# Newton statistics of a Stieltjes attention placed in PSUM instead of SBUF

## The chip, the cores and the metric

The kernel runs on one core of a Trainium2 chip, in one launch. The metric is the device time of that launch in microseconds (us); before the change it is 5724.81 us, the median of three runs (5724.38 to 5730.4).

## What is computed

The reference has two parts that follow each other. `x` is 8 sequences of 512 tokens with 128 channels, all in float32.

```python
x = x + _L0_attn_ref(_layernorm(x), Wqkv, Wo)        # first part: 16 heads of 8 channels
x = x + _L0_ffn_ref(_layernorm(x), ...)              # second part: 6 layers, local attention and MLP
...
def stieltjes_attention(Q, K, V, scale, causal, q, num_iter):   # q = 1, num_iter = 4
    s = jnp.einsum('bhnd,bhmd->bhnm', Q, K) * scale
    s_masked = jnp.where(mask, s, -1e+30)
    lam = s_masked.max(-1) + 1.0
    for _ in range(num_iter):
        d = jnp.maximum(lam[..., None] - s, EPS)
        w = jnp.where(mask, d ** (-q), 0.0)
        f = w.sum(-1) - 1.0
        fp = -q * jnp.where(mask, d ** (-q - 1.0), 0.0).sum(-1)
        lam = lam - f / fp
    d = jnp.maximum(lam[..., None] - s, EPS)
    p = jnp.where(mask, d ** (-q), 0.0)
    p = p / p.sum(-1, keepdims=True)
    return jnp.einsum('bhnm,bhmd->bhnd', p, V)
```

So each row of the scores needs a root of `sum(1/(lam - s)) = 1`, found with four Newton steps. A step needs two sums over the row: that of `w = 1/d` and that of `w*w`. Only the first part is touched by the change.

## The kernel before

The kernel is written for a tile framework. The program text gives the work in an order of priority; a scheduler decides at build time in which order each engine gets its instructions, and puts semaphore waits where two instructions touch the same data. For tiles in PSUM it takes two accesses to one bank of a tile as touching each other, whichever columns they use. The order on an engine is then fixed, and the engine works through it in sequence.

**The first part** works on blocks of 128 rows of one sequence. A block `rb` (0 to 3) sees `W = (rb + 1) * 128` columns. Blocks are taken in pairs, (3, 0) and (2, 1), so 16 pairs in all for 8 sequences. A pipeline over the pairs has three stages: while the pair `nxt` gets its scores, the pair `now` gets its Newton steps and the pair `before` gets its weights and sums of V. In each turn the loops over `k` (4 Newton steps) and `u` (the two blocks of a pair) call, in this order, `attend_add` (L264), `scores` (L195), `newton` (L225), `attend_sum` of the turn before (L275) and `attend_weigh` (L269). There are 16 x 4 x 2 = 128 calls of `newton` and 128 of `attend_sum`.

- `scores` makes a score tile with TensorE (L204), and VectorE adds the mask and takes the row minimum (L209); L215 and L217 make the distances `ns` in SBUF.
- `newton` makes `w` for four groups `j` of four heads: ScalarE takes Ln (L234, L237 or L241) and Exp with scale -1 (L242) into `d`, a pool of two buffers. For the narrow blocks GpSimd adds the growth `dl` of `lam` first (`add_growth`, L222). VectorE then takes `bn_stats` of each head (L244): 16 a call, each writing count, mean and sum of squared deviations for the even and the odd elements, six numbers. L249 to L260 turn them into the new `dl` with eight or nine small VectorE instructions on 16 or 32 elements for each partition; the ninth (L259) runs only for `k > 0`, so 3 calls in 4.
- `attend_add` is again the GpSimd line L222, on a tile `da`; `attend_weigh` makes the weights (ScalarE L269, L270) and masks the diagonal (GpSimd L272).
- `attend_sum` transposes the weights with TensorE (L286), copies them to SBUF with VectorE (L288, `dT`, one copy for each of four heads), multiplies with V on TensorE (L293) into a PSUM tile `po` with a bank of its own, and copies that out with VectorE (L297). A block with `nkb = rb + 1` column blocks has `4 * nkb` such multiplications; the profile shows two matmuls for each[...].

All operands of L249 to L260 lie in SBUF before the change. The eight PSUM banks of the first part are taken: four for scores, two for transposes, one for projections, one for `po`.

**The second part** (from L326 on) runs the six layers. Nothing in it changes.

Of the kernel before, what the change touches and what calls it, by code (L numbers as in the profile page):

```python
# [9 lines left out]
F32 = mybir.dt.float32  # L10
BF16 = mybir.dt.bfloat16
AF = mybir.ActivationFunctionType
ALU = mybir.AluOpType
AX = mybir.AxisListType
PSUM = bass.MemoryType.PSUM

P = 128
N = 512
# [4 lines left out]
H = 16  # L23
# [26 lines left out]
def tile_kernel(  # L50
# [18 lines left out]
    nc = tc.nc  # L69
# [20 lines left out]
    def normalized_T(pool, ppool, b, dst):  # L90

        st = pool.tile([P, NT, 6], F32, name="st")
        mv = pool.tile([P, NT, 2], F32, name="mv")
        for c in range(NT):
            nc.vector.bn_stats(st[:, c, :], x2[:, b, c, :])
            nc.vector.bn_aggr(mv[:, c, :], st[:, c, :])
        rstd = pool.tile([P, NT], F32, name="rstd")
        nc.scalar.activation(rstd, mv[:, :, 1], AF.Ln, bias=eps_ln)
        nc.scalar.activation(rstd, rstd, AF.Exp, scale=-0.5)
        xn = pool.tile([P, NT, D], F32, name="xn", bufs=1)  # L100
        pt = ppool.tile([P, N], F32, name="pt", tag="misc")
        for c in range(NT):
            nc.vector.tensor_scalar(
                xn[:, c, :], x2[:, b, c, :], mv[:, c, 0:1], rstd[:, c : c + 1],
                ALU.subtract, ALU.mult,
            )
            nc.tensor.transpose(pt[:, c * P : (c + 1) * P], xn[:, c, :], ident)
        nc.scalar.copy(dst, pt)


    with ExitStack() as c1:
# [5 lines left out]
        sm = c1.enter_context(tc.tile_pool(name="sm", bufs=4))  # L117
# [3 lines left out]
        ps_o = c1.enter_context(tc.tile_pool(name="ps_o", bufs=1, space=PSUM))  # L121
# [99 lines left out]
        def add_growth(d, ns, dl, j):  # L221
            nc.gpsimd.tensor_tensor(  # L222
                d, ns, dl[:, 4 * j : 4 * j + 4].unsqueeze(2).to_broadcast(list(d.shape)), ALU.add
            )

        def newton(t, k):
            W, dl = t["W"], t["dl"]

            st = sm.tile([P, H, 2, 3], F32, name="stw")
            for j in range(4):  # L230
                ns = t["ns"][j]
                d = dp.tile([P, 4, W], F32, name="d", tag="d")
                if k == 0:
                    nc.scalar.activation(d, ns, AF.Ln)  # L234
                elif W <= 2 * P:
                    add_growth(d, ns, dl, j)
                    nc.scalar.activation(d, d, AF.Ln)  # L237
                else:
                    for g in range(4):
                        i = 4 * j + g  # L240
                        nc.scalar.activation(d[:, g, :], ns[:, g, :], AF.Ln, bias=dl[:, i : i + 1])  # L241
                nc.scalar.activation(d, d, AF.Exp, scale=-1.0)  # L242
                for g in range(4):
                    nc.vector.bn_stats(st[:, 4 * j + g].rearrange("p u k -> p (u k)"), d[:, g, :])  # L244

            hw = float(W // 2)
            mean = st[:, :, :, 1]
            q2 = sm.tile([P, H, 2], F32, name="q2")
            nc.vector.scalar_tensor_tensor(q2, mean, hw, mean, ALU.mult, ALU.mult)  # L249
            nc.vector.tensor_tensor(q2, q2, st[:, :, :, 2], ALU.add)  # L250
            sw2 = sm.tile([P, H], F32, name="sw2")
            nc.vector.tensor_tensor(sw2, q2[:, :, 0], q2[:, :, 1], ALU.add)
            sw = sm.tile([P, H], F32, name="sw")
            nc.vector.tensor_tensor(sw, mean[:, :, 0], mean[:, :, 1], ALU.add)
            nc.vector.tensor_scalar(sw, sw, hw, -1.0, ALU.mult, ALU.add)
            nc.vector.reciprocal(sw2, sw2)
            nc.vector.tensor_tensor(sw, sw, sw2, ALU.mult)
            if k > 0:
                nc.vector.tensor_tensor(sw, sw, dl, ALU.add)  # L259
            nc.vector.tensor_scalar(dl, sw, 0.0, None, ALU.max)  # L260

        def attend_add(t, j):

# [13 lines left out]
        def attend_sum(t, d, j):  # L277

            nkb, (qj, kn, va) = t["nkb"], t["proj"]
            if j == 0:  # L280
                t["o4"] = bt.tile([P, 4, P], F32, name="o4")
            dT = []
            for g in range(4):
                pt = ps_t.tile([P, nkb, P], F32, name="dTp", tag="t")
                for kb in range(nkb):
                    nc.tensor.transpose(pt[:, kb, :], d[:, g, kb * P : (kb + 1) * P], ident)  # L286
                dT.append(tr.tile([P, nkb, P], F32, name="dT", tag="dT"))
                nc.vector.tensor_copy(dT[g], pt)  # L288

            po = ps_o.tile([P, P], F32, name="po")  # L290
            for kb in range(nkb):
                for g in range(4):
                    nc.tensor.matmul(  # L293
                        po[32 * g : 32 * g + 32, :], lhsT=va[:, kb, 4 * g + j, :],
                        rhs=dT[g][:, kb, :], start=(kb == 0), stop=(kb == nkb - 1),
                    )
            nc.vector.tensor_copy(t["o4"][:, j, :], po)  # L297
            if j == 3:
                attend_end(t)
                if t["rb"] == 1:  # L300
                    normalized_T(bt, ps_m, t["b"], xT[:, t["b"], :])

        def attend_end(t):
            b, rb, o4 = t["b"], t["rb"], t["o4"]
            pq = ps_m.tile([P, 4, 4, 32], F32, name="pq4", tag="misc")
            for j in range(4):
                nc.tensor.transpose(pq[:, j].rearrange("p g r -> p (g r)"), o4[:, j, :], ident)
            den = sm.tile([P, 4, 4], F32, name="den")
            nc.vector.reciprocal(den, pq[:, :, :, DH])
            o = bt.tile([P, H, DH], F32, name="o")  # L310
            nc.vector.tensor_tensor(
                o.rearrange("p (g j) d -> p j g d", j=4), pq[:, :, :, 0:DH],
                den.unsqueeze(3).to_broadcast([P, 4, 4, DH]), ALU.mult,
            )
            pT = ps_m.tile([P, P], F32, name="pT", tag="misc")
            nc.tensor.transpose(pT, o.rearrange("p h d -> p (h d)"), ident)
            oT = bt.tile([P, P], F32, name="oT")
            nc.scalar.copy(oT, pT)
            pr = ps_m.tile([P, P], F32, name="pr", tag="misc")
            nc.tensor.matmul(pr, lhsT=oT, rhs=wT[:, 3, :], start=True, stop=True)  # L320
            nc.vector.tensor_tensor(x2[:, b, rb, :], x2[:, b, rb, :], pr, ALU.add)
# [10 lines left out]
        for w in range(len(work) + 1):  # L332
            before, now, nxt = now, nxt, []
            if w + 1 < len(work):
                b, rbs = work[w + 1]
                nxt = [block(b, rb, proj) for rb in rbs]
            for k in range(NUM_ITER):
                for u in range(2):
                    if before:
                        attend_add(before[u], k)  # L340
                    if nxt:
                        scores(nxt[u], k)
                    if now:
                        newton(now[u], k)
                    if ready:
                        attend_sum(*ready)
                        ready = None
                    if before:
                        attend_weigh(before[u])
                        ready = (before[u], before[u]["d"], k)  # L350
            if w + 2 < len(work) and work[w + 2][1][0] == 3:
                if ready:
                    attend_sum(*ready)
                    ready = None
                proj = project(work[w + 2][0])
        attend_sum(*ready)


# [354 lines left out]
    while t < len(halves) * PH + LAG or parts:  # L713
        i, p = t // PH, t % PH
        a = done = ahead = None
        if 0 <= i < len(halves):
            a = dict(g=groups[i], p=p)
# [87 lines left out]
```

## Time and profile before

| what | value |
|---|---|
| median of three runs | 5724.81 us |
| the profiled execution's own time | 5724.38 us |
| its span, first to last instruction | 5722.4 us |
| busy share over the span: TensorE, VectorE, ScalarE, GpSimd | 82%, 83%, 71%, 57% |
| first part, about 0 to 2060 us: last Newton step's end | 2062.7 us |
| `bn_stats` L244: count, busy in the whole first part | 2048, 871 us (four shapes) |
| L249 to L260: instructions | 1120 |

PE stands for TensorE, DVE for VectorE, ACT for ScalarE, POOL for GpSimd. In the views of groups each row names line, engine, operation, the tile written and the tile read, shapes and count; behind the bar stand the busy time in us and the mean duration in ns, then the idle time just before, with what ended it. In a timeline a row is the start in us, the length in us, and the instructions; rows of several instructions are runs of equal ones, and a row can start before the one ahead of it has ended, because instructions overlap a little in the engine.

### The profile page before, as it was taken

What the parts mean: (1) busy time and instruction counts of PE and PEld (TensorE: products, weight loads), DVE (VectorE), ACT (ScalarE), POOL (GpSimd) and SP (SyncE); (2) the same over time, 40 slices, a digit from 0 to 9 for tenths busy, and PEclk for the clock granted to TensorE, in tenths of its full rate; (3) what the DMA queues carried; (4) which work ended last, traced back from release to release, by engine and by line L of the source; (5) the groups of instructions that cost most, each with busy time, mean ns of one, the idle gap of its engine ahead of it and who ended that gap; (6) DMA issues with size and microseconds to landing.
All of it is one profiled execution on the core that took longest, in us unless ns stands there. A gap on an engine that the chain in (4) does not pass through costs nothing.

```text
span 5722.4 us, 108133 instructions
## 1 busy us (share of the span) xinstructions
PE 4686.3 (82%) x40909; PEld 2744.5 (48%) x40909; DVE 4775.5 (83%) x12028; ACT 4038.0 (71%) x6458; POOL 3250.3 (57%) x2915
## 2 busy tenths in 40 slices
PE   4556566655666549999999999999999999999998
PEld 2223333332333225556656555555555655556665
DVE  8889898998989858888888888888888888888886
ACT  5788888888888856666666666666666666666665
POOL 1333233333323347777777677777777777777774
PEclk6555555555555569999999999999999999999999
DMA  0000000000000011111111211122111111121111
GB/s 17 1 0 1 1 1 1 1 1 0 1 1 1 1 39 44 44 47 47 46 44 42 58 47 40 39 51 53 44 44 44 52 44 42 47 58 45 47 42 34
DMA packets 106558, 173.16 MB, mean 30 GB/s; under 512 B 12816, under 2 KB 30008, under 8 KB 106040
## 3 DMA queue, kind: packets, MB, share of 16 engines
q1 hardware_dynamic: 106040, 166.25, 11.7%
q8 instruction: 325, 5.32, 0.4%
q14 instruction: 193, 1.58, 0.1%
HBM read 19.42 MB, written 2.10 MB: 4 GB/s over the span
## 4 chain that ended last, share of the span: by engine, by line
PE 39%; DVE 33%; ACT 20%; POOL 5%; issue 2%; DMA 0%; SPq 0%; POOLq 0%; ACTq 0%; DVEq 0%
DVE stw L244 9%; PE m L476 8%; PE po L594 4%; PE pT L584 4%; PE pv L512 4%; PE s L559 3%; ACT d L241 3%; ACT d L242 3%; DVE qr L492 3%; ACT qT L540 3%; DVE ss L482 3%; PE acc L607 3%; DVE rs L572 3%; DVE qn L484 3%; DVE ns L209 2%
## 5 line engine op out<-in xcount | busy, mean ns | idle before, releaser
L496 POOL TENSOR_TENSOR qn<-qn,qr 128x512 f32<-128x512 f32 x768 | 975.5, 1271 | 580.4 <-DVE qr L492 430.0
L244 DVE BATCH_NORM_STATS2 stw<-d 128x6 f32<-128x512 f32 (+3 forms) x2048 | 868.1, 476 | 76.7 <-ACT d L242 74.8
L504 POOL TENSOR_TENSOR qn<-qn,ss 128x512 f32<-128x512 f32 x768 | 784.6, 1042 | 40.5 <-ACT ss L501 36.8
L482 DVE TENSOR_REDUCE ss<-sq 128x8 f32<-128x512 f32 x768 | 522.2, 680 | 328.5 <-ACT sq L481 326.0
L574 POOL TENSOR_TENSOR pr<-pr,rs 128x768 f32<-128x768 f32 x384 | 564.0, 1469 | 382.9 <-DVE rs L573 249.1
L476 PE MATMUL m<-wqkv,xs 128*128 128x512 f32 x1536 | 738.4, 603 | 48.2 <-ACT qT L540 37.6
L222 POOL TENSOR_TENSOR d<-ns,dl 128x512 f32<-128x512 f32 (+1 forms) x192 | 288.1, 1500 | 641.6 <-DVE stw L244 388.8
L242 ACT ACTIVATE d<-d 128x1536 f32<-128x1536 f32 (+3 forms) x512 | 641.3, 1261 | 5.3
L204 PE MATMUL s<-kn,qj 32*128 32x512 f32 (+3 forms) x1024 | 420.0, 753 | 245.5 <-DVE mn L209 242.0
L572 DVE TENSOR_REDUCE rs<-pr 128x8 f32<-128x768 f32 x384 | 364.8, 950 | 287.7 <-ACT pr L570 287.5
L222 POOL TENSOR_TENSOR da<-ns,dl 128x2048 f32<-128x2048 f32 (+3 forms) x128 | 299.1, 2340 | 502.4 <-PE dTp L286 362.1
L492 DVE TENSOR_TENSOR qr<-m,tab 128x256 f32<-128x256 f32 x1536 | 571.2, 413 | 0.0
L286 PE MATMUL dTp<-ident,da 128*128 128x128 f32 x1280 | 382.4, 424 | 221.5 <-ACT da L270 107.4
L481 ACT ACTIVATE sq<-m 128x512 f32<-128x512 f32 x768 | 439.3, 601 | 129.3 <-PE m L476 83.1
L601 ACT COPY oT<-po 128x512 f32<-128x512 f32 x384 | 223.8, 583 | 413.5 <-PE po L594 407.9
L484 DVE TENSOR_TENSOR qn<-m,tab 128x512 f32<-128x512 f32 x768 | 514.7, 670 | 0.0
L540 ACT COPY qT<-ptq 128x512 f32<-128x512 f32 x768 | 416.5, 583 | 90.6 <-PE ptq L535 90.0
L585 ACT COPY prT<-pT 96x512 f32<-96x512 f32 x768 | 431.5, 584 | 62.6 <-PE pT L584 53.5
L293 PE MATMUL po<-dT,va 128*32 128x128 f32 x2560 | 333.5, 395 | 173.1 <-DVE dT L288 173.0
L535 PEld LDWEIGHTS ptq<-ident,qn 128*128 128x128 f32 x3072 | 358.8, 141 | 220.0 <-issue 111.5
L241 ACT ACTIVATE d<-ns,dl 128x512 f32<-128x512 f32 (+1 forms) x768 | 450.6, 654 | 14.2 <-DVE stw L244 14.2
L584 PE MATMUL pT<-ident,pr 128*96 128x128 f32 x3072 | 411.6, 274 | 55.8 <-DVE rs L573 46.2
(137 smaller groups left out, 9910.0 us busy)
## 6 DMA issues: line engine op xcount, KB each, us to landing
v<-v SPq DMA_DIRECT2D x192, 512.0 KB
v<-v SPq DMA_DIRECT2D x96, 256.0 KB
v<-v SPq DMA_DIRECT2D x96, 192.0 KB
wqkv<-in_L_ffn_Wqkv_dram SPq DMA_DIRECT2D x36, 256.0 KB
wo<-in_L_ffn_Wo_dram SPq DMA_DIRECT2D x12, 256.0 KB
x<-in_L_attn_x_dram SPq DMA_DIRECT2D x8, 256.0 KB
out_dram<-x SPq DMA_DIRECT2D x8, 256.0 KB
w<-in_L_ffn_W_dram SPq DMA_DIRECT2D x6, 341.0 KB
```

The lines of the kernel that those rows point to most:

```text
L222: nc.gpsimd.tensor_tensor(d, ns, dl[:, 4 * j : 4 * j + 4].unsqueeze(2).to_broadcast(list(d.shape)), ALU.add)
L241: nc.scalar.activation(d[:, g, :], ns[:, g, :], AF.Ln, bias=dl[:, i : i + 1])
L242: nc.scalar.activation(d, d, AF.Exp, scale=-1.0)
L244: nc.vector.bn_stats(st[:, 4 * j + g].rearrange("p u k -> p (u k)"), d[:, g, :])
L476: nc.tensor.matmul(m.rearrange("p h e -> p (h e)"), lhsT=lhsT, rhs=wqkv[:, t, :], start=True, stop=True,)
L482: nc.vector.tensor_reduce(ss[:, t, :], sq, axis=AX.X, op=ALU.add)
L484: nc.vector.tensor_tensor(qc, m, tab[:, 2 * t, c, :].unsqueeze(1).to_broadcast([P, HH, DHL]), ALU.mult)
L492: nc.vector.tensor_tensor(qr[:, :, u, :], mh[:, :, 1 - u, :], sw.unsqueeze(1).to_broadcast([P, HH, hd]), ALU.mult,)
L496: nc.gpsimd.tensor_tensor(qc, qc, qr.rearrange("p h u e -> p h (u e)"), ALU.add)
L504: nc.gpsimd.tensor_tensor(qc, qc, ss[:, t, :].unsqueeze(2).to_broadcast([P, HH, DHL]), ALU.mult)
L540: nc.scalar.copy(q, pt)
L584: nc.tensor.transpose(pT[:, c, :], pr[:, e, c, :], ident)
```

## The change

One PSUM tile `small` of a full bank (512 numbers for each partition) is allocated once, in the pool that held `po`. Its first 128 columns are `po`. Behind them lie two sets of statistics `st` and of two rows `r`, which calls of `newton` use in turn. `bn_stats` writes to `st` in PSUM. The small instructions are rewritten so that none has two tensor operands in SBUF, and none has two in PSUM: a copy of the means to SBUF comes first, the sums over the even and odd halves are reductions, and the reciprocal and the step go to `r` in PSUM. The number of small instructions stays at eight, nine for `k > 0`. The formulas are scaled by `1/hw` but give the same step.

```diff
+        small = ps_o.tile([P, N], F32, name="small")
+        po = small[:, 0:P]
+        stats, turn, c0 = [], 0, P
+        for u in range(2):
+            st = small[:, c0 : c0 + 6 * H].rearrange("p (h u k) -> p h u k", u=2, k=3)
+            r = small[:, c0 + 6 * H : c0 + 8 * H].rearrange("p (a h) -> p a h", h=H)
+            stats.append((st, r))
+            c0 += 8 * H
+
         def newton(t, k):
+            nonlocal turn
             W, dl = t["W"], t["dl"]
 
-            st = sm.tile([P, H, 2, 3], F32, name="stw")
+            turn = (turn + 1) % 2
+            st, r = stats[turn]
...
             hw = float(W // 2)
-            mean = st[:, :, :, 1]
-            q2 = sm.tile([P, H, 2], F32, name="q2")
-            nc.vector.scalar_tensor_tensor(q2, mean, hw, mean, ALU.mult, ALU.mult)
-            nc.vector.tensor_tensor(q2, q2, st[:, :, :, 2], ALU.add)
+            mean, m2 = st[:, :, :, 1], st[:, :, :, 2]
+            q = sm.tile([P, H, 2], F32, name="q2")
+            nc.vector.tensor_copy(q, mean)
+            nc.vector.tensor_tensor(q, mean, q, ALU.mult)
+            nc.vector.scalar_tensor_tensor(q, m2, 1.0 / hw, q, ALU.mult, ALU.add)
             sw2 = sm.tile([P, H], F32, name="sw2")
-            nc.vector.tensor_tensor(sw2, q2[:, :, 0], q2[:, :, 1], ALU.add)
+            nc.vector.tensor_reduce(sw2, q, axis=AX.X, op=ALU.add)
+            nc.vector.reciprocal(r[:, 0], sw2)
             sw = sm.tile([P, H], F32, name="sw")
-            nc.vector.tensor_tensor(sw, mean[:, :, 0], mean[:, :, 1], ALU.add)
-            nc.vector.tensor_scalar(sw, sw, hw, -1.0, ALU.mult, ALU.add)
-            nc.vector.reciprocal(sw2, sw2)
-            nc.vector.tensor_tensor(sw, sw, sw2, ALU.mult)
+            nc.vector.tensor_reduce(sw, mean, axis=AX.X, op=ALU.add)
+            nc.vector.scalar_tensor_tensor(
+                r[:, 1], sw, -1.0 / hw, r[:, 0], ALU.add, ALU.mult
+            )
             if k > 0:
-                nc.vector.tensor_tensor(sw, sw, dl, ALU.add)
-            nc.vector.tensor_scalar(dl, sw, 0.0, None, ALU.max)
+                nc.vector.tensor_tensor(r[:, 1], r[:, 1], dl, ALU.add)
+            nc.vector.tensor_scalar(dl, r[:, 1], 0.0, None, ALU.max)
...
-            po = ps_o.tile([P, P], F32, name="po")
```

In the changed file `bn_stats` is line L256, the small instructions are L261 to L274, the copies `dT` L302, the multiplications with V L306 and the copy out of them L310.

## The prediction

> **What bounds the kernel now.** I first read the slices of the page: VectorE is busy 8 or 9 tenths from the start to about 2060 us, where the Newton steps end. The view of one stage says it in sums:
>
> ```profile
> core 0: us, PE busy (x) PEld busy (x) DVE busy (x) ACT busy (x) POOL busy (x), PEclk, DMA share, GB/s
> 60.00:2060.00 2000.00, 1148.38 (x4899) 574.83 (x4897) 1780.25 (x5586) 1647.57 (x1913) 653.99 (x446) 0.54 0.00 1
> ```
>
> VectorE (DVE) works 1780 of 2000 us, ScalarE (ACT) 1648, TensorE (PE) 1148. So this stage is VectorE's, and what lengthens VectorE's queue lengthens the kernel, unless one of its waits shrinks. Its waits in the same stretch:
>
> ```profile
> DVE stw L244 <- ACT d L242: 74.8, 72, 4.6
> DVE o L297 <- PE po L293: 43.6, 50, 2.0
> DVE ns L209 <- POOL da L222: 26.7, 16, 2.1
> DVE dT L288 <- PE dTp L286: 21.4, 32, 3.2
> ```
>
> The columns are us in total, times, and the longest; all of them come to about 210 us. Next, VectorE's groups by shape, for the small instructions:
>
> ```profile
> L257 DVE TENSOR_TENSOR sw<-sw,sw 128x16 f32<-128x16 f32 x128 | 55.8, 436 | 0.3
> L250 DVE TENSOR_TENSOR q<-q,stw 128x32 f32<-128x32 f32 x128 | 55.4, 433 | 0.0
> L254 DVE TENSOR_TENSOR sw<-stw 128x16 f32<-128x16 f32 x128 | 54.7, 427 | 0.0
> L249 DVE SCALAR_TENSOR_TENSOR q<-stw 128x32 f32<-128x32 f32 x128 | 33.6, 262 | 0.6
> L256 DVE RECIPROCAL sw<-sw 128x16 f32<-128x16 f32 x128 | 29.9, 233 | 0.2
> ```
>
> An add of 16 elements takes 427 ns in the mean, a reciprocal of 16 only 233. The view of each line gives the reason: L254 has minimum, median and maximum of 169, 179 and 1911 ns, L256 194, 232 and 253. Some adds with two SBUF operands are held for up to 2 us, about as long as one addition of GpSimd (POOL) at L222 lasts (median 1522 ns on `d`, 2422 ns on `da`). The one-operand reciprocal never is. This is what the change can win.
>
> Last, the timeline of VectorE, for the price of a dependence:
>
> ```profile
> 2041.36 1.94 DVE L244 BATCH_NORM_STATS2 stw<-d 128x6 f32<-128x384 f32 x4 [1.09 <-ACT d L242]
> 2043.34 0.20 DVE L249 SCALAR_TENSOR_TENSOR q<-stw 128x32 f32<-128x32 f32 x1
> 2043.45 0.18 DVE L254 TENSOR_TENSOR sw<-stw 128x16 f32<-128x16 f32 x1
> ...
> 2061.72 0.24 DVE L256 RECIPROCAL sw<-sw 128x16 f32<-128x16 f32 x1
> 2062.00 0.17 DVE L257 TENSOR_TENSOR sw<-sw,sw 128x16 f32<-128x16 f32 x1
> 2062.20 0.18 DVE L259 TENSOR_TENSOR sw<-sw,dl 128x16 f32<-128x16 f32 x1
> ```
>
> L249 needs the last `bn_stats`: it starts 0.04 us after that one's end (2043.30). L257 needs L256 and again starts 0.04 us after its end. L254 needs nothing of L249 and starts 0.09 us before L249's end. So an instruction that waits for the one right ahead of it costs **0.13 us** more than one that doesn't. The four `bn_stats` in the first row overlap in this way: 1.94 us for four of 0.55 us.
>
> [...] 128 elements take 276 ns from SBUF (L244) and 278 from PSUM (L288). A VectorE write to PSUM isn't in this trace. [...]
>
> **The change, part by part.** I also read the built order of the changed program, engine by engine, with the value that each instruction waits for.
>
> *The hold by GpSimd.* L249 to L260 are busy 349.7 us together (sum of their nine rows). At their medians (191, 199, 161, 179, 165, 232, 158 and 159 ns, x128, and 163 ns x96) they would take 200.4. So 149.3 us are holds. None of L261 to L274 has two SBUF inputs, or both its source and its output in SBUF except one reduction: all of it goes. **-149 us.**
>
> *The small instructions themselves.* With the overlap of 0.08 us in most pairs, 1120 old ones cost 200.4 - 89.6 = 110.8 us. The new ones, by the nearest rows: four on 32 elements at 191 (copy, L263, both reductions), L262 at 199, reciprocal 232, L269 at 179, L274 at 159, L273 at 163 (x96): 211.9 - 89.6 = 122.3 us. But in before the scheduler laid them between other instructions; now 1046 of 1120 wait for the one right ahead: 1046 x 0.13 = 136. Sum 258.3 against 110.8: **+148 us.** The chain so gives back what the hold cost.
>
> *`bn_stats` to PSUM.* In before none of the 2048 waits for VectorE. Now all write one bank, so nearly each waits for the one before. For 881 of them that is the instruction right ahead (225, 268, 197 and 191 of the shapes 512, 384, 256 and 128); the others have an L209, L217 or L302 in between and lose nothing. 881 x 0.13 = **+115 us.** About 90 such pairs of the old order are gone: **-12 us.**
>
> *The shared bank.* `po` now lies in the bank of the statistics. In 113 of 128 calls the multiplications L306 wait for L274, the end of a Newton step, and the copy L310 stands only one instruction behind it on VectorE, with the next call's `bn_stats` queued behind L310. In before L293 waited for its `dT` alone, and mostly four `bn_stats` lay between. How long TensorE needs:
>
> ```profile
> 1028.62 1.92 PE L293 MATMUL po<-dT,va 128*32 128x128 f32 x26
> ...
> 1030.57 0.29 DVE L297 COPY o<-po 128x128 f32<-128x128 f32 x1 [0.47 <-PE po L293]
> ```
>
> Runs of 10, 18 and 26 take 1.06, 1.49 and 1.92 us, so 0.43 for each 8. For 8, 16, 24 and 32 I get 0.96, 1.38, 1.81 and 2.23, and 0.10 for the way to TensorE and back. The one copy `dT` between covers 0.60, 0.46, 0.33 and 0.20 us. Stall: 31 x 0.46 + 22 x 1.02 + 28 x 1.58 + 25 x 2.13; 7 more have four L209 (1.37 us) to cover 2.33, 7 x 0.96: together 141 us. The wait of 43.6 us at L297 is part of that: **+97 us.** Behind L306 in TensorE's queue stand the next transposes and scores; they come later by the same wait, but TensorE has 850 us free here and two transposed tiles are ready before it, so I cost that at nothing; if this cover fails, the wait for `dTp` (21 us) grows.
>
> *What shrinks, and what shifts.* VectorE comes later to its other waits. I take half of the wait for ACT (37) and a third of those for POOL and `dTp` (16): **-53 us.** GpSimd's additions still run, and may now hold L217 or L215 in place of the chain: between 0 and half of the 149; L217 and L215 lose about 36 us to it today, so I take **+15 us.**
>
> Sum: -149 + 148 + 115 - 12 + 97 - 53 + 15 = **+161 us**. Against the profiled execution's 5724.4 us (span 5722.4, 2 around it; the median of the runs, 5724.8, is the same) this gives 5885 us. The second part, from 2060 us on, is not touched.
>
> *Unknown: the write to PSUM.* It could signal its end earlier or later than one to SBUF. [...] I take zero for both, since the rows of 276 and 278 ns show no difference.
>
> **The rivals.** (A) *A dependence costs nothing*[...]. Then 251 us of the sum go: 161 - 251 = -90, 5634 us, **faster**. It decides at 90 / 1927 = 0.047 us for a pair; above that the change loses. For it: no VectorE write to PSUM is in the trace. Against: 0.13 us at every waiting pair that I looked up. (B) *ScalarE runs dry.* The pool `d` has two buffers. During chain and stall (about 4 us) ScalarE fills both and stops; then VectorE takes a tile of 2048 in 4 x 0.73 = 2.9 us, where ScalarE needs 2 x 1.89 = 3.8 (L234 and L242). Two tiles in each of 64 wide steps: 64 x 2 x 0.9 = 115 us more, 6000 us. For it: L244's wait for ACT is the longest of VectorE's now. Against: scores and copies lie between the tiles. (C) *The slack takes it.* All 166 us of other waits shrink to nothing in place of 53: +48, 5772 us. (D) *The holds stay*, on these or other instructions: 161 + 149, 6034 us. Against it: the never held reciprocal.
>
> **How the numbers follow.** My sum 0.70, A 0.07, B 0.11, C 0.09, D 0.03. Likeliest 5885. The range reaches down to C[...], 5750, and up to B, 6000; this leaves out A, D and part of B. A measurement can tell about 0.2% (11 us) from no change: faster 0.07, same 0.03, slower 0.90.
>
> **What would show it.** Right: L261 to L274 without maxima over 0.4 us; runs of `bn_stats` at 0.73 us a piece of 512 in place of 0.60; L310 with about 140 us of idle time ahead of it, ended by TensorE; GpSimd's rows unchanged. Wrong: `bn_stats` runs at 0.60 as before (A), the wait for ACT grown to 150 us or more (B) or gone (C), or L217 with means far over today's (D). The prediction fails in sign if the dependent pairs are cheaper than 0.05 us.

## The result, and the profile after

The changed kernel takes 6098.8 us (median of four runs, 6098.05 to 6100.56) against 5724.6 us for four runs of the kernel before: a ratio of 1.0652, with a 95% interval of 1.0633 to 1.0670. It is slower by 374 us. I had forecast slower, by 161 us, with a range that ended at 6000.

The view of the first part's stretch in the changed kernel, whose last Newton step ends at 2437 us in place of 2063:

```profile
core 0: us, PE busy (x) PEld busy (x) DVE busy (x) ACT busy (x) POOL busy (x), PEclk, DMA share, GB/s
60.00:2430.00 2370.00, 999.18 (x4829) 573.66 (x4827) 1842.53 (x5552) 1690.90 (x1910) 648.67 (x446) 0.56 0.00 1
```

The stretch is 370 us longer than that of before (60 to 2060 us) and VectorE is busy only 62 us longer; 308 us are new idle time of VectorE. From the end of the last Newton step on, the second part took 3661 us, against 3660 before. VectorE's waits in this stretch:

```profile
DVE small L256 <- ACT d L254: 169.5, 145, 4.7
DVE dT L302 <- PE small L306: 140.3, 105, 2.0
DVE ns L209 <- POOL da L222: 57.5, 58, 2.1
DVE x L334 <- PE pr L333: 40.5, 25, 3.3
```

The first was 74.8 us before, the third 26.7. The second is the stall at the shared bank. The small instructions and a shape of `bn_stats`, from VectorE's groups by shape:

```profile
L262 DVE TENSOR_TENSOR q<-small,q 128x32 f32<-128x32 f32 x128 | 24.3, 190 | 3.8
L266 DVE RECIPROCAL small<-sw 128x16 f32<-128x16 f32 x128 | 33.4, 261 | 4.4
L215 DVE TENSOR_SCALAR lam<-mn 128x4 f32<-128x4 f32 x128 | 55.5, 434 | 0.0
L256 DVE BATCH_NORM_STATS2 small<-d 128x6 f32<-128x512 f32 x512 | 356.5, 696 | 68.8 <-ACT d L254 61.4
```

The last two of these were, before:

```profile
L215 DVE TENSOR_SCALAR lam<-mn 128x4 f32<-128x4 f32 x128 | 31.3, 245 | 0.1
L244 DVE BATCH_NORM_STATS2 stw<-d 128x6 f32<-128x512 f32 x512 | 317.6, 678 | 23.1 <-ACT d L242 21.8
```

The change does what it says: L262 takes 190 ns in the mean (its maximum is 192), where L250 took 433. The idle time of about 4 us ahead of each small group is new; it is 128 times the gap of 34 ns (median) between an instruction and the one that waits for it. L215, with its operands still in SBUF, went from 245 to 434 ns in the mean. Its median hardly moved (154 to 160), but 21 of the 128 now take over 0.9 us, where 2 did before, and all of these overlap an addition of GpSimd at L222. I read this as part of the hold by GpSimd that moved there. The `bn_stats` of 512 went from 678 to 696 ns.

VectorE's timeline shows the new order:

```profile
1020.33 2.91 DVE L256 BATCH_NORM_STATS2 small<-d 128x6 f32<-128x512 f32 x4 [1.48 <-ACT d L254]
1023.27 0.19 DVE L261 COPY q<-small 128x32 f32<-128x32 f32 x1
...
1025.12 0.17 DVE L274 TENSOR_SCALAR dl<-small 128x16 f32<-128x16 f32 x1
1026.45 0.56 DVE L302 COPY dT<-dTp 128x384 f32<-128x384 f32 x1 [1.15 <-PE small L306]
1026.92 0.28 DVE L310 COPY o<-small 128x128 f32<-128x128 f32 x1
```

Four `bn_stats` of 512 take 2.91 us (2.47 before), then come nine small instructions in a block of 2.0 us with nothing between them, then a stall of 1.15 us until TensorE has done the multiplications with V, and only then the next call's `bn_stats`. In before the small instructions lay between other work, `bn_stats` of the next call among it:

```profile
1011.02 0.41 DVE L244 BATCH_NORM_STATS2 stw<-d 128x6 f32<-128x256 f32 x1
1011.36 0.18 DVE L250 TENSOR_TENSOR q<-q,stw 128x32 f32<-128x32 f32 x1
1011.46 0.17 DVE L255 TENSOR_SCALAR sw<-sw 128x16 f32<-128x16 f32 x1
1011.54 0.42 DVE L244 BATCH_NORM_STATS2 stw<-d 128x6 f32<-128x256 f32 x1
1011.88 0.15 DVE L252 TENSOR_TENSOR sw<-q 128x16 f32<-128x16 f32 x1
```

Here the call's own `bn_stats` were those of 384 elements; those of 256 belong to the next call.

TensorE at the stall, and the waits of the other engines in the same stretch:

```profile
1003.18 1.50 PE L306 MATMUL small<-dT,va 128*32 128x128 f32 x24 [5.01 <-DVE dl L274]
```

```profile
PE small L306 <- DVE dl L274: 1008.8, 112, 15.8
POOL d L222 <- DVE small L256: 697.2, 142, 88.0
POOL da L222 <- PE dTp L300: 658.1, 88, 31.9
ACT da L283 <- POOL da L222: 252.8, 100, 5.3
```

The multiplications now start in one block at the end of a Newton step, after 1009 us of waiting for it in all. The other three lines were 389, 355 and 40 us in the stretch from 60 to 2060 us of before.

### The profile page after: what moved, and what is told of

Same layout as the page of the kernel before. It is cut to its first block, busy times and chain, and to the rows that moved or that the text cites. A ratio compares the mean times of both kernels' runs of the same rounds, so it can differ in the third digit from the quotient of the medians.

```text
span 6097.4 us, 108471 instructions
## 1 busy us (share of the span) xinstructions
PE 4546.4 (75%) x40909; PEld 2749.6 (45%) x40909; DVE 4846.0 (79%) x12028; ACT 4084.6 (67%) x6458; POOL 3248.3 (53%) x2915
## 4 chain that ended last, share of the span: by engine, by line
PE 37%; DVE 29%; ACT 24%; POOL 7%; issue 3%; DMA 0%; SPq 0%; POOLq 0%; DVEq 0%; ACTq 0%
PE m L489 8%; DVE small L256 7%; PE po L607 4%; PE pT L597 4%; PE pv L525 4%; ACT d L254 4%; POOL da L222 4%; ACT d L253 4%; PE s L572 3%; DVE qr L505 3%; ACT qT L553 3%; DVE ss L495 3%; PE acc L620 2%; DVE rs L585 2%; DVE qn L497 2%
## 5 line engine op out<-in xcount | busy, mean ns | idle before, releaser
L256 DVE BATCH_NORM_STATS2 small<-d 128x6 f32<-128x512 f32 (+3 forms) x2048 | 1017.1, 497 | 207.2 <-ACT d L254 173.8
L306 PE MATMUL small<-dT,va 128*32 128x128 f32 x2560 | 171.0, 412 | 1021.3 <-DVE dl L274 1021.3
L222 POOL TENSOR_TENSOR da<-ns,dl 128x2048 f32<-128x2048 f32 (+3 forms) x128 | 297.0, 2321 | 769.3 <-PE dTp L300 661.8
L222 POOL TENSOR_TENSOR d<-ns,dl 128x512 f32<-128x512 f32 (+1 forms) x192 | 282.5, 1472 | 707.8 <-DVE small L256 697.2
L306 PEld LDWEIGHTS small<-dT,va 128*32 128x32 f32 x2560 | 102.0, 158 | 1115.3 <-DVE dl L274 1101.7
L204 PE MATMUL s<-kn,qj 32*128 32x256 f32 (+3 forms) x1024 | 450.3, 804 | 185.2 <-DVE mn L209 181.5
```

Source lines behind the costliest of these rows:

```text
L222: nc.gpsimd.tensor_tensor(d, ns, dl[:, 4 * j : 4 * j + 4].unsqueeze(2).to_broadcast(list(d.shape)), ALU.add)
```

## The experiments

Two theories to begin with. **S**: the bank shared with the sums of V is the main cost, by its stall and through TensorE's blocked queue. **D**: the steps have become longer chains and ScalarE runs dry on two `d` buffers. (This D is the prediction's rival B again, not its rival D.) In the first four runs a control and three variants were compared. A ratio is against the kernel before, run again on the same chip: its median there was 5744.5 us for these four runs, 5723.4 us for the four of the next group ("A bank for each turn" and the first of "Where else q and r can lie"), and 5726.2 us for the last four. So differences between groups, and from the changed kernel's own 6098.8 us, are sure to some 20 us only.

### A control, and a bank of its own

To free a bank, the scores get three buffers in place of four.

```diff
-        ps_s = c1.enter_context(tc.tile_pool(name="ps_s", bufs=4, space=PSUM))
+        ps_s = c1.enter_context(tc.tile_pool(name="ps_s", bufs=3, space=PSUM))
```

> The kernel before with three PSUM buffers for scores in place of four, so that a bank is free: the control for runs that give the statistics a bank of their own. Both theories: 5725 to 5770 us, since the scores' wait for L209 on TensorE lies beside VectorE's work; it says what the missing buffer costs.

Measured: 5751.7 us, ratio 1.0019 (1.0012 to 1.0025). The lost buffer costs 7 us by the medians and 11 us by the ratio.

The next run keeps the changed kernel but for the bank:

```diff
-        small = ps_o.tile([P, N], F32, name="small")
-        po = small[:, 0:P]
+        ps_n = c1.enter_context(tc.tile_pool(name="ps_n", bufs=1, space=PSUM))
+        small = ps_n.tile([P, N], F32, name="small")
...
+            po = ps_o.tile([P, P], F32, name="po")
```

> The changed kernel, but the statistics have a bank of their own (three score buffers) and the sums of V have theirs as before, so that no multiplication with V waits for a Newton step. Theory S (the shared bank is the main cost: its own stall of about 97 us, and through TensorE's blocked queue the later transposes, weights and Exp): 5770 to 5850 us, VectorE's wait for ScalarE back to 60 to 100 us; what is left over the control is the dependent bn_stats (881 x 0.13 = 115 us) and the dependent small ones, less the hold of 149. Theory D (ScalarE runs dry since the steps are longer chains on two d buffers, whatever bank): over 5950 us, with that wait still at 150 us or more.

Measured: 6007.8 us, ratio 1.0463 (1.0447 to 1.0478): only 91 us come back, about 100 with the lost buffer allowed for. VectorE's waits in its first part:

```profile
DVE small L256 <- ACT d L254: 163.8, 147, 4.5
DVE o L311 <- PE po L307: 112.2, 107, 3.4
DVE dT L302 <- PE dTp L300: 63.7, 90, 7.8
```

In the control the first of these was 80.0 us:

```profile
DVE stw L244 <- ACT d L242: 80.0, 77, 4.6
```

The wait for ScalarE stays at 164 us although no multiplication with V waits for a Newton step any more. Theory S falls as the main cause; D's numbers hold so far.

### More buffers for the weights

```diff
-            d = t["d"] = dp.tile([P, 4, t["W"]], F32, name="da", tag="da", bufs=3)
+            d = t["d"] = dp.tile([P, 4, t["W"]], F32, name="da", tag="da" + str(int(t["rb"] < 2)), bufs=2)
```

> The changed kernel with the weights' tiles da in two tags of two buffers each (wide and narrow blocks) in place of three buffers for both, in the same SBUF space. Theory S (TensorE's blocked queue frees da late, so GpSimd and with it ScalarE wait): GpSimd's wait for the transposes falls from 658 us to under 400, ScalarE's wait for da from 253 to about 100, the time to 5960 to 6030 us. Theory D (the two d buffers): 6080 to 6120 us, no change.

Measured: 6093.8 us, ratio 1.0613 (1.0588 to 1.0638), which overlaps the changed kernel's interval: no clear change. GpSimd still waits 642 us for the transposes. ScalarE's wait for `da` did fall, from 253 to 159 us, yet VectorE's wait for ScalarE rose from 170 to 200. So the way through late `da` tiles, the second half of S, isn't shown; late `da` was not what held the kernel.

### Statistics in SBUF, only q and r in PSUM

```diff
+            st = sm.tile([P, H, 2, 3], F32, name="stw")
...
-            st = small[:, c0 : c0 + 6 * H].rearrange("p (h u k) -> p h u k", u=2, k=3)
+            q = small[:, c0 : c0 + 2 * H].rearrange("p (h u) -> p h u", u=2)
```

> The statistics stay in SBUF as before; only the small intermediate tiles q and r lie in PSUM, in a bank of their own (three score buffers), so that no small instruction has two SBUF operands. bn_stats no longer waits for bn_stats, and nothing on TensorE waits for a Newton step. If the hold by GpSimd is worth its 149 us: 100 to 140 us below the control, 5590 to 5650 us. If the holds move on to other instructions of VectorE: within 40 us of the control.

Measured: 5677.3 us, ratio 0.9893 (0.9874 to 0.9911): 74 us under its control, less than the 100 to 140 expected, and 331 us under the run that differs from it only in where the statistics lie. In its trace only 27 `bn_stats` start within 0.12 us after the end of the instruction ahead (772 in the run with the own bank); nearly all others overlap it or wait longer. The small instructions are interleaved again. VectorE's wait for ScalarE, 164 us with the statistics in PSUM, is here:

```profile
DVE stw L257 <- ACT d L255: 106.5, 109, 4.4
```

So most of the cost comes with the statistics in PSUM, with or without the bank shared. This gave the third theory, **L**: all 16 `bn_stats` and the small instructions of all calls write to one bank, so a call's `bn_stats` must follow the whole of the call before (the line-up); rival **W**: a write to PSUM or a dependent pair is dearer than I took it.

### A bank for each turn, and the line-up in SBUF

The control for two free banks has two score buffers.

> The kernel before with two score buffers in place of four: the control for the next run, which needs two free banks. From what the loss of one buffer did (5748 to 5758 us): 5750 to 5850 us.

Measured: 5817.2 us, ratio 1.0160 (1.0139 to 1.0181).

```diff
         for u in range(2):
+            small = ps_n.tile([P, N], F32, name=f"small{u}")
             st = small[:, c0 : c0 + 6 * H].rearrange("p (h u k) -> p h u k", u=2, k=3)
```

> The changed kernel with the statistics of even and odd calls of newton in two banks of their own (two score buffers), and the sums of V as before. A call's bn_stats then need not follow the small instructions of the call before. In its built order 349 bn_stats wait for the one right ahead, in place of 923 in the run with one own bank, and the small instructions are interleaved again. Theory L (the line-up of one call behind the other, through the one bank, is the main cost, and ScalarE's two d buffers run full meanwhile): within 0 to 80 us of its control (349 x 0.13 = 45 us for the pairs, less part of the hold), with VectorE's wait for ScalarE near 80 to 110 us. Theory W (a write to PSUM or a dependent pair costs more than 0.13 us by itself): 150 us or more over the control.

Measured: 5846.1 us, ratio 1.0211 (1.0196 to 1.0227): 29 us over its control, where one bank stood 256 us over its own. VectorE's wait for ScalarE, in the control and then here:

```profile
DVE stw L244 <- ACT d L242: 85.0, 74, 4.6
```

```profile
DVE small L256 <- ACT d L254: 116.4, 127, 5.2
```

With alternate banks nearly all of the loss is gone, as L said. The second bank removes two things at once, though: the line-up, and more than half of the dependent `bn_stats` (340 start within 0.12 us after the one ahead, 772 with one bank). At 0.126 us each, the latter are some 54 of the 227 us.

The other way round: the kernel before, all in SBUF, but with one buffer for a call's statistics and rows.

```diff
-            st = sm.tile([P, H, 2, 3], F32, name="stw")
+            whole = sm.tile([P, H, 8], F32, name="stw", bufs=1)
+            st = whole[:, :, 0:6].rearrange("p h (u k) -> p h u k", u=2)
...
-            sw2 = sm.tile([P, H], F32, name="sw2")
+            sw2 = whole[:, :, 6]
...
-            sw = sm.tile([P, H], F32, name="sw")
+            sw = whole[:, :, 7]
```

> The kernel before, all in SBUF, with one buffer for a call's statistics that also holds the rows sw and sw2, so that a call's bn_stats must wait for the whole of the small instructions of the call before; in the built order only 98 bn_stats wait for the one right ahead. The hold by GpSimd stays. Theory L: 100 to 250 us over the kernel before, VectorE's wait for ScalarE up from 75 to 130 us or more. Theory W: within 40 us of the kernel before.

Measured: 5816.8 us, ratio 1.0160 (1.0143 to 1.0177): 93 us over before, just under L's range and far over W's. The waits of VectorE in its first part:

```profile
DVE stw L245 <- ACT d L243: 150.5, 103, 5.6
DVE o L298 <- PE po L294: 65.1, 67, 2.0
```

No PSUM, no dependent `bn_stats` to speak of (58 start within 0.12 us after the one ahead), and yet the wait for ScalarE doubles from 75 to 151 us. This is the wait that had grown in the changed kernel too (170) and that I had expected to shrink. Busy time and short gaps of VectorE are only 6 us more than before here; the loss is all in longer waits.

### Where else q and r can lie

The first of these puts them in the bank of the projections and of a block's end, with four score buffers.

```diff
+            small = ps_m.tile([P, 4 * H], F32, name="small", tag="misc")
+            q = small[:, 0 : 2 * H].rearrange("p (h u) -> p h u", u=2)
```

> Statistics in SBUF, the intermediate tiles q and r in the PSUM bank of the projections and of the end of a block, so that four score buffers stay. If that bank is free at most calls: 5640 to 5680 us, at or under the run with q and r in a bank of their own (5677). If the small instructions often wait for the end of a block there: 5700 to 5800 us.

Measured: 5701.8 us, ratio 0.9959 (0.9944 to 0.9974), at the lower edge of the second case, but not for its reason: the small instructions hardly wait there (0.5 us in all, by the view of their tile). It is the transposes at the end of a block (L312) that wait for them, 157 us on TensorE. VectorE waits 174 us for ScalarE.

The second is one part of the change alone, the bank shared with the sums of V, with the statistics back in SBUF. Its edit puts `st` in SBUF and `q` in PSUM by the lines of "Statistics in SBUF, only q and r in PSUM", and leaves `small` and `po` in one bank:

> One part of the change alone: q and r lie in the bank of the sums of V as in the changed kernel (so the multiplications with V still wait for the end of a Newton step, in 113 of 128 calls), but the statistics stay in SBUF, so that bn_stats waits neither for bn_stats nor for the small instructions of the call before. Four score buffers. If the line-up of calls is what makes the change slow (theory L): the hold's gain (about 75 us in the run with a bank of its own) against a stall of some 90 us that other bn_stats can now partly cover: 5680 to 5780 us. If the blocked queue of TensorE is the main cost (theory S): over 5850 us.

Measured: 5717.0 us, ratio 0.9980 (0.9973 to 0.9988). Its waits, VectorE's first, TensorE's second:

```profile
DVE stw L257 <- ACT d L255: 174.9, 162, 3.7
DVE o L310 <- PE small L306: 30.7, 38, 1.3
DVE dT L302 <- PE small L306: 19.8, 17, 2.0
```

```profile
PE small L306 <- DVE dl L274: 513.8, 92, 14.3
```

The multiplications wait 514 us for the Newton steps, but on VectorE only 51 us of stall at them are left (144 in the changed kernel), since the next call's `bn_stats` can run meanwhile. The shared bank alone is bearable; with the statistics in it, it isn't: 382 us lie between this run and the change. VectorE's wait for ScalarE is no lower than in the change (175 against 170), although the kernel is so much faster. A long wait alone does not tell what is lost: VectorE has less to do here.

The third frees a bank by giving the sums of V a turn in the two buffers of the transposes:

```diff
-            po = ps_o.tile([P, P], F32, name="po")
+            po = ps_t.tile([P, P], F32, name="po", tag="t")
```

> Statistics in SBUF, q and r in a bank of their own, and the sums of V in the two buffers of the transposes, so that four score buffers stay. If the sums seldom hold up a transpose: 5640 to 5675 us, under the run with three score buffers (5677). If they do: 5690 us or more, with longer waits of VectorE for dTp.

Measured: 5643.1 us (5642.4 to 5643.9), ratio 0.9855 (0.9838 to 0.9871). It beats both kernels. Three of its groups:

```profile
L262 DVE TENSOR_TENSOR small<-stw,small 128x32 f32<-128x32 f32 x128 | 24.6, 192 | 0.0
L215 DVE TENSOR_SCALAR lam<-mn 128x4 f32<-128x4 f32 x128 | 43.1, 337 | 0.3
L217 DVE TENSOR_SCALAR ns<-ns,lam 128x512 f32<-128x512 f32 x128 | 81.0, 669 | 0.0
```

No small instruction is held (the longest of all nine lines is 261 ns), and none of the lines has more than 0.6 us of idle time ahead of it. L217 at 669 ns (567 before) and L215 at 337 (245 before) show what I take to have become of the hold: over all shapes the two lines are about 45 us longer, of the 149.

### Are the buffers of d what carries the line-up?

> The kernel with calls in line in SBUF (one buffer for statistics, sw and sw2), with the weights in two wide and one narrow buffer and four buffers for dT, which frees the space that the next run needs. A control: 5800 to 5870 us.

Measured: 5798.1 us, ratio 1.0126 (1.0105 to 1.0146).

```diff
-                d = dp.tile([P, 4, W], F32, name="d", tag="d")
+                d = dp.tile([P, 4, W], F32, name="d", tag="d" + str(int(t["rb"] < 2)))
```

> As the control, with two more buffers for d (two wide and two narrow ones in place of two for both), so that ScalarE can go on into the next call while VectorE is in the small instructions. If the full buffers of d carry the cost of the line-up: 40 to 90 us under the control, VectorE's wait for ScalarE at 100 us or less. If not: within 20 us of the control.

Measured: 5782.1 us, ratio 1.0098 (1.0072 to 1.0124), 16 us under its control, with 18 us between its own two runs. VectorE's wait for ScalarE did not fall; it was 162 us in the control, and here:

```profile
DVE stw L245 <- ACT d L243: 189.8, 113, 4.7
```

The two `d` buffers carry little or nothing of it, so theory D, as I had put it, is not supported. The test was made on the kernel with calls in line in SBUF, not on the changed kernel itself.

## Why the prediction was wrong in size

The sign was right. A sum over VectorE's first part up to the end of the last Newton step, made instruction by instruction from the traces, splits it into busy time, gaps under 0.12 us and longer waits (us; the last column is the part of the waits that ScalarE ended at `bn_stats`):

| run | busy | short gaps | longer waits | of these, for ScalarE |
|---|---|---|---|---|
| before | 1825 | 7 | 231 | 76 |
| changed | 1889 | 75 | 472 | 174 |
| three score buffers (control) | 1819 | 7 | 261 | 81 |
| own bank | 1866 | 61 | 417 | 165 |
| statistics in SBUF, own bank | 1720 | 8 | 283 | 109 |
| two score buffers (control) | 1846 | 9 | 299 | 86 |
| a bank for each turn | 1818 | 26 | 345 | 118 |
| calls in line in SBUF | 1821 | 17 | 314 | 151 |
| shared bank alone | 1708 | 10 | 339 | 177 |

From before to the change this is +64 of busy time, +68 of short gaps and +241 of longer waits, 374 in all before rounding. For the steps, each instruction is given the time by which it moves the end of VectorE's work on, longer waits left out:

- **The hold, -149:** right. In before, 134 instructions of L249 to L260 take over 0.25 us more than the median of their line, 149 us in sum; each of them overlaps an instruction of GpSimd and ends within 0.1 us after the end of one (40 ns in the median). 16 of them are L255 and L260, which have one tensor operand. The hold is gone from all nine lines: none of the new ones has an instruction over 261 ns, though 334 of the 1120 overlap GpSimd.
- **The small instructions, +148:** right: a dependent one starts 34 ns after the end of the one ahead, an independent one 80 to 90 ns before it, in PSUM as in SBUF. Block and hold cancel: together these two steps measure -17 us, forecast -1.
- **`bn_stats`, +115 less 12:** right in kind, too low in size: measured +142. The built order has 881 that wait for the one right ahead, with a start 117 ns later (34 ns after the end of the one ahead in place of 83 ns before it) and some 9 ns of longer duration: 111 us. What I had put at zero, the unknown of the write to PSUM, is the rest, and only in part a slower write. Among `bn_stats` that start after a wait, one into PSUM takes about 8 ns longer (512 elements: 694 to 702, 128 elements: 294 to 302, medians). When the instruction behind it is independent, that one starts about 91 ns before its end instead of 81, so little is lost there. What is left is not split further.
- **The hold that shifts, +15:** right in sum, about 13 us over L215, L217 and L103.
- **The shared bank, +97:** measured 144 us of stall against 141 forecast, +101 with the 44 of before taken off. This is luck, since two errors cancel. The one copy `dT` ahead of L310 gives no cover: in 105 places it waits for a multiplication L306 itself (the stall stands at L302 in the waits above). And the multiplications are quicker in one block than I worked out: 1.93 us for 32 and 1.51 for 24, in place of 2.23 and 1.81.

The terms so far come to +214 (-149 + 148 + 115 - 12 + 15 + 97), against about +233 measured for them (64 + 68 + 101); of the 19 between, `bn_stats` are +39 and the small instructions -16. **The step that failed is "what shrinks, and what shifts": I took 53 us off the other waits, and they grew by 140.** ScalarE's grew by 98, L209's by 35 (31 of it for GpSimd), that of the residual add L334 by 29; the one for `dTp` fell by 13 and the rest by 8. Between -53 and +140 lie 193 us, nine tenths of the miss of 213. I reasoned that a VectorE that comes later meets work that is done earlier. But here the order itself changed. With all calls' statistics in one bank, one call's small instructions can no longer lie between the next call's `bn_stats`. I had read this in the built order ("interleaved" there, one block here) and priced only its pairs.

That a line-up of calls can raise these waits is shown by the run that imposes it in SBUF: busy time and short gaps grow by 6 us, longer waits by 83, and 75 of these are for ScalarE. Lifting it in PSUM by a second bank agrees: over the controls, the growth of the wait for ScalarE falls from 84 to 32 us and the loss from 256 to 29, part of it through fewer dependent pairs. In the pair with an own bank, the difference between statistics in PSUM and in SBUF splits into 147 of busy time, 53 of gaps and 134 of longer waits.

How much of the 193 us in the changed kernel is the line-up's is not shown. With the statistics in SBUF and the shared bank kept, 382 us go, but not through the wait for ScalarE, which stays at 177: it is 181 of busy time, 65 of gaps and 134 of waits, and of the waits 97 are the stall at the shared bank. So the same wait of VectorE for ScalarE also comes without any line-up of `bn_stats`, where VectorE has less to do. The three columns have to be read together.

The prediction's rivals: A falls, a dependence costs in PSUM what it does in SBUF (a start 34 ns after the end of the one ahead in both). C and D did not come. The 22 us by which my range went below C, for the write to PSUM, were an estimate that no trace showed. B named the sign that came (the wait for ScalarE at 150 us or more), but its mechanism, two full `d` buffers, got no support from the last pair of runs. "I cost that at nothing" for the work behind L306 did not show in the wait that I had named for it: the wait for `dTp` fell, and more `da` buffers gained nothing.

**What stays open:** by which way the line-up makes VectorE wait for ScalarE. GpSimd's wait for `bn_stats` at L222 rises from 389 to 697 us in the changed kernel, and ScalarE's wait for the weights from 40 to 253. More `da` buffers in the changed kernel, or more `d` buffers in the one with calls in line, don't cure it. Every variant is also scheduled anew, so the order on all engines differs from run to run of the table; what part such an order has by chance, and what a better fixed order would do, was not tried. Nor were dependent `bn_stats` tried alone: their 111 us are read from the traces, not from a run of their own.

## What to carry to other kernels

When a tile moves to PSUM in this framework, its dependences are counted by the bank (here L306 waited 112 times for L274, which uses other columns, 1009 us in all). Look in the built order for instructions that now wait for the one right ahead, and for calls that can no longer overlap, before pricing what the move saves. Here the gain was real (5643 us in the best run) and needed only the small intermediate tiles in PSUM. The large stream of writers should have stayed in SBUF, where calls have buffers of their own (5677 us against 6008, with an own bank in both). Of the three places tried for the small tiles with four score buffers, a bank that no other engine's queue depends on was the best (5643 us against 5702 and 5717). And if a change reorders an engine's queue, don't assume that its other waits shrink by the time added: check whether independent work that used to cover them is still allowed there.

## What the runs showed of the hardware beyond expectation

- A `bn_stats` that writes to PSUM takes about 8 ns longer than one to SBUF at all four sizes, where both start after a wait (medians: 694 to 702 ns at 512 elements, 560 to 569 at 384, 428 to 435 at 256, 294 to 302 at 128). The medians of those that overlap differ by 18 ns, but they compare unlike neighbours: before, most stand behind another `bn_stats`, and in the changed kernel behind another kind of instruction. In SBUF too, one behind another kind takes about 10 ns longer (685 against 675 at 512 elements).
- A `bn_stats` with two waits, for the VectorE instruction ahead and for ScalarE, has the first of them in a semaphore instruction of its own. Where ScalarE was done in time, it starts 103 ns after the end of the one ahead (median of 88 such cases in the changed kernel, all sizes), not 34; in SBUF, in the run with calls in line, it is 103 ns too (41 cases). L274 with two waits starts at 107 ns (48 cases).
- Taking the hold by GpSimd from the small instructions seems to remove it only in part: in the best version about 45 us of the 149 stand on L215 and L217, `tensor_scalar` lines from SBUF to SBUF (337 and, at 512 elements, 669 ns in the mean, 245 and 567 before).
